# Two-layer masked attention on one core: layer 0's softmax sums counted once per half, layer 1's first accumulating DMA issued two steps later

## The chip, the cores and the metric

The kernel runs on one core of a Trainium2 chip. The metric is the device time of one execution in microseconds (us). The core has five engines with queues of their own, which work side by side and wait for one another through semaphores: TensorE (PE: matmuls; PEld is its weight load), VectorE (DVE), ScalarE (ACT), GpSimd (POOL) and SyncE (SP). In this kernel SP issues the plain DMAs, and GpSimd issues the loads of the adjacency matrix and the DMAs that add while they copy.

## What is computed

Sixteen graphs of 1024 nodes with 256 features go through two layers. Each layer normalizes its input, applies a ReLU, and adds masked attention to the input: 4 heads of 64 features in layer 0, 8 heads of 32 in layer 1. All is float32.

```python
# layer 0 (layer 1: 8 heads of 32, the same adjacency, with biases)
h = jnp.maximum(_layernorm(x, axis=-1), 0.0)
Q, K, V = ...                                   # per head
scores = jnp.einsum('bhne,bhme->bhnm', Q, K) * scale
scores = jnp.where(mask, scores, -jnp.inf)
attn = jax.nn.softmax(scores, axis=-1)
heads = jnp.einsum('bhnm,bhme->bhne', attn, V)
x = x + concat(heads) @ Wo.T + bo
```

## The kernel before

**Tiling.** For one graph and layer the 1024 queries fall into two halves of 512 (`qh`). The heads fall into two groups (`g`): a group holds 128 features, so two heads in layer 0 and four in layer 1. A group of a half is worked in steps, 4 in layer 0 and 8 in layer 1. A step computes four blocks of 128 keys x 512 queries: `scores` (TensorE, L447, into PSUM tiles `ps`), then `exponentials`: a mask operation on VectorE (L463) and an exponential on ScalarE (L469), giving the tile `p`; then, two steps later, `weigh` (TensorE, L481) multiplies `p` with the values into `po`. Layer 0 thus has 16 steps a graph and layer 1 has 32. The whole program is one list of 768 steps: layer 0 of graph b+1, then layer 1 of graph b, and so on. Below, *a* is the step at which layer 0 of a graph begins and *c* = a + 16 the one at which layer 1 of the graph before it begins.

**The sums of the softmax.** The exponentials are not divided by their sum at once. Tiles of a group are added up (layer 0: `add_tiles`, L490 to L496, on VectorE and GpSimd; layer 1: GpSimd, L582, for two tiles, and DMAs that add one pair into the other, `accumulate`, L568). Then `count` (L343) multiplies the result with ones on TensorE. This sums over the 128 partitions and leaves the sums of each head in `pz`, repeated over the head's rows. Layer 0 counts once a group, two matmuls of 64 columns; layer 1 counts a group in two counts, each four matmuls of 32 columns. After that come, by due times counted in steps from the end of the group:

- `spread`: ScalarE copies `pz` to `s`; small DMAs on SP deal a row of each head out over partitions (`sums`);
- `invert`: VectorE takes the reciprocal `vn` (L383), and a DMA puts it into DRAM (`vd`);
- `fetch`: DMAs on SP read it back, repeated over the rows of a head (`inv`);
- `normalize`: GpSimd multiplies the weighted values `cat` with `inv` (L399);
- `end_half`, after both groups: TensorE multiplies `cat` with the output weights (`py`, L429), and VectorE adds the rows (L434).

**What sets the order.** The order on each engine is written out by hand. `Stream.run` goes through the steps; in each it issues the scores of this step, the weighing of the step two earlier (put off by one step, where an even step has a large matmul block due), the counts due, the exponentials, the additions of layer 0, and then the other work due, in the order in which it was entered, with the large matmul blocks (`k`, `q`, `values`, `end_half`) last. `later(i, f)` enters work for step i. Every engine then runs its own queue in order. As GpSimd and SP wait only for what they need, they can be ahead of the step that TensorE is at, or behind.

For a layer 0 group that ends at step i, the count and the spread are due at i+4, then invert i+6, fetch i+7, normalize i+9, end_half i+11. The end is two steps after the last step's own number, so in a graph's layer 0 the counts fall at a+9, a+13, a+17 and a+21. In layer 1 the first accumulating DMA of a group is issued at the step of its fourth tile (`j == 3`), and the first count follows `waits[0]` steps later; in the first group that is the DMA at c+5 and the count at c+11.

**Buffers.** Three pairs of PSUM banks serve `ps`, `pq`, `pv` and `py` in turn, so that a new one waits for the reader of the one three back. Odd tiles `p` have two buffers and even ones seven: a mask operation of an odd step waits for the GpSimd addition (L582) that reads the tile two odd steps back. `pz` has one bank.

Of the kernel before, what the change touches and what calls it, by code (L numbers as in the profile page):

```python
# [10 lines left out]
F32 = mybir.dt.float32  # L11
# [7 lines left out]
P = 128  # L19
# [69 lines left out]
def fast_program(ctx, tc, a, w, loads, chk):  # L89
# [3 lines left out]
    nc = tc.nc  # L93
# [8 lines left out]
    work = ctx.enter_context(tc.tile_pool(name="work", bufs=2))  # L102
# [209 lines left out]
    class Group:  # L312


        def __init__(self, inp, mask, qh, g, half):
            self.inp, self.mask, self.qh, self.g, self.half = inp, mask, qh, g, half
            self.layer = inp.layer
            self.D = E // HEADS[self.layer]
            self.per = P // self.D
            self.scale = 1.0 / math.sqrt(self.D)  # L320
            self.n = f"{inp.n}_{qh}_{g}"
            self.n_f = self.per * 512 // P
            self.last = qh == QH - 1 and g == 1

            self.hurry = False

            self.waits = ((6, 6), (7, 7), (8, 6), None)[2 * qh + g]

            self.brief, self.pairs = self.last and inp.b == B - 2, False

# [7 lines left out]
        def count(self, p, start, stop):  # L338

            if start:  # L340
                self.s = ps_o.tile([P, 512], F32, tag="pz", name=f"pz_{self.n}")
            for r in range(self.per):
                nc.tensor.matmul(  # L343
                    self.s[r * self.D : (r + 1) * self.D, :], w.ones.to_broadcast([P, self.D]), p[:, r, :],
                    start=start, stop=stop,
                )

        def count_added(self):
            self.count(self.t, True, True)

        def copy_out(self):
            if self.g == 0:
# [5 lines left out]

        def spread(self):

            s = work.tile([P, 512], F32, tag="s", bufs=1, name=f"s_{self.n}")
            nc.scalar.copy(tiled(s), by_tile(self.s))  # L362
            inp, k = self.inp, 2 * self.qh + self.g
            if k == 0:

                pool, tag = small, f"sums{self.layer}"
                if self.layer and inp.b == B - 1:
                    pool, tag = adjp, "adj"
                inp.sums = pool.tile(
                    [P, 4 * self.n_f], F32, tag=tag, bufs=1, name=f"sums_{inp.n}"  # L370
                )
            self.sn = inp.sums[:, ts(k, self.n_f)]
            lanes = P // self.per
            for r in range(self.per):
                nc.sync.dma_start(
                    self.sn[r * lanes : (r + 1) * lanes, :],
                    s[r * self.D : r * self.D + 1, :].rearrange("r (c f) -> r c f", f=self.n_f),
                )

        def invert(self):  # L380

            vn = small.tile([P, self.n_f], F32, tag="vn", bufs=1, name=f"vn_{self.n}")
            nc.vector.reciprocal(vn, self.sn)  # L383
            vd = dram.tile([self.per, 512], F32, tag=f"vd{self.layer}", name=f"vd_{self.n}")
            nc.sync.dma_start(self.lanes(vd), vn)
            self.vd = vd

        def fetch(self):

            vd = self.vd  # L390
            self.inv = work.tile([P, 512], F32, tag="inv", bufs=1, name=f"inv_{self.n}")
            for r in range(self.per):
                nc.sync.dma_start(
                    self.inv[r * self.D : (r + 1) * self.D, :], vd[r].partition_broadcast(self.D)
                )

        def normalize(self):
            o = self.half.cat[:, self.g, :]
            nc.gpsimd.tensor_mul(o, o, self.inv)  # L399

        def finish(self):

            inp, qh = self.inp, self.qh
            inv = work.tile([P, 512], F32, tag="inv", bufs=1, name=f"inv_{self.n}")
            py = psum_pair(f"py_{self.n}").rearrange("p a (t e) -> p (a t) e", e=E)
            rows, cat = xs[inp.b, qh], self.half.cat
            dst = quarters(out, inp.b, qh)
            for h in range(2):
                q = ts(h, 256)
                nc.vector.reciprocal(tiled(inv)[:, ts(h, 2)], by_tile(self.s)[:, ts(h, 2)])  # L410
                nc.vector.tensor_mul(cat[:, self.g, q], cat[:, self.g, q], inv[:, q])
                for i in (2 * h, 2 * h + 1):
                    for c in range(2):
                        nc.tensor.matmul(
                            py[:, i, :], cat[:, c, ts(i, P)], w.o[self.layer][:, c, :],
                            start=(c == 0), stop=(c == 1),
                        )
            for h in range(2):
                t = ts(h, 2)
                nc.vector.tensor_add(rows[:, t, :], py[:, t, :], rows[:, t, :])  # L420
                for g in range(4):
                    nc.sync.dma_start(dst[g][:, t, :], rows[ts(g, 32), t, :])
# [84 lines left out]
    class Stream:  # L507
# [62 lines left out]
        def count_steps(self, i, st):  # L570


            gr, j = st.gr, st.j
            if gr.hurry and j >= NT - 2:
                if st.last:
                    self.counted(i, gr)
                gr.count(st.p, False, st.last)
            elif j % 2:
                one = self.steps[i - LEAD - 1].p
                if gr.last and not (gr.brief or gr.pairs) and j == 7:  # L580
                    self.accumulate(gr.two, gr.one)
                nc.gpsimd.tensor_add(one, one, st.p)  # L582
                if gr.pairs:
                    self.later(i + 2, gr.count, one, j == 1, st.last)
                elif j == 1:
                    gr.one = one
                elif j == 3:
                    self.accumulate(one, gr.one)
                    gr.one = one
                    if not gr.last:  # L590
                        self.later(i + gr.waits[0], gr.count, one, True, False)
                    if gr.brief:
                        self.later(i + 8, gr.count, one, True, False)
                elif gr.brief:
                    self.later(i + (6 if j == 5 else 4), gr.count, one, False, st.last)
                elif j == 5:
                    gr.two = one
                elif not gr.last:
                    self.accumulate(one, gr.two)
                    self.later(i + gr.waits[1], gr.count, one, False, True)  # L600
                else:
                    self.later(i + 1, self.accumulate, one, gr.two)
                    self.later(i + 4, gr.count, one, True, True)
# [7 lines left out]
        def end_group(self, i, gr):  # L611

            if gr.hurry:
                for f in (gr.spread, gr.finish, gr.inp.test):
                    self.later(i, f)
                return

            if gr.layer == 0:
                self.later(i + 4, gr.count_added)
                at = 4, 6, 7, 9, 11  # L620
            else:
                at = ((6, 12, 15, 19), (7, 12, 14, 17, 19), (6, 9, 11, 14), None)[2 * gr.qh + gr.g]
                if gr.pairs:
                    at = 2, 5, 6, 7, 9
                elif gr.last:
                    at = 4, 6, 7, 9, 11
            for k, f in zip(at, (gr.spread, gr.invert, gr.fetch, gr.normalize)):
                self.later(i + k, f)
            if gr.last:

                k = 7 if gr.layer or gr.inp.b == 0 else 37
                self.later(i + k if gr.inp.b + gr.layer < B - 1 else len(self.steps) + 2, gr.inp.test)
            if gr.g == 1:
                self.later(i + at[4], gr.end_half)
# [109 lines left out]
    for t in range(NT):  # L744
        i = 5 + 2 * t
# [8 lines left out]
    for b in range(B - 1):  # L754
# [14 lines left out]
        if b + 2 < B:  # L769
# [3 lines left out]
            if b == 0:  # L773
                norms(other, 0, a + 14, a + 15, c + 2, c + 3)
                block_inputs(other, 0, c + 4, c + 5, c + 6, c + 8, c + 16, c + 18)
                norms(other, 1, c + 3, c + 4, c + 6, c + 7)
                block_inputs(other, 1, c + 10, c + 12, c + 16, c + 22, c + 26, c + 30)
            else:
                norms(other, 0, a + 10, a + 12, a + 13, a + 15)
                block_inputs(other, 0, c, c + 1, c + 2, c + 8, c + 16, c + 18)  # L780
                norms(other, 1, c, c + 4, c + 5, c + 6, bias=c + 42)
                block_inputs(other, 1, c + 7, c + 8, c + 12, c + 22, c + 26, c + 30)
            for i, t in zip((9, 13, 17, 22, 33, 37, 41, 45), range(NT)):
                later(a + i - 5, mask.load, t)
# [260 lines left out]
```

## Time and profile before

| | |
|---|---|
| median of 3 runs | 3202.38 us (3201.98 to 3203.7) |
| profiled execution | 3201.31 us, of which the span of the core is 3199.5 us |
| granted TensorE clock | 0.997 of full speed |
| scores, L447 (PE) | 1134.1 us busy, 6144 matmul entries |
| weighing, L481 (PE) | 990.6 us busy, 6144 entries |
| counts, L343 (PE) | 196.1 us busy, 1248 entries |
| mask operation, L463 (DVE) | 1796.8 us busy, 1536 of 1212 ns |
| addition of two tiles, L582 (POOL) | 1171.3 us busy, 255 of 4596 ns |
| normalization, L399 (POOL) | 185.4 us busy, 127 of 1460 ns |
| issue of an accumulating DMA, L568 (POOL) | 133 of 882 ns (median) |

A row of the profile's groups reads: line, engine, operation, output<-input, shapes, count | busy us, mean ns of one | idle time of the engine just before, and what ended it. A row of a timeline reads: start in us, length, engine, line, operation, with the idle time before it and its releaser in square brackets. The times of matmuls overlap, since one begins before the last has drained, so what a block of them costs is read from the start of the next.

### The profile page before, as it was taken

The numbers are of one execution on the slowest core, as the hardware profiler recorded it, in microseconds if no ns is written. First come the engines' busy times: TensorE is split into PE (matmuls) and PEld (weight loads), VectorE is DVE, ScalarE is ACT, GpSimd is POOL, SyncE is SP. The second block draws the span as 40 slices with busy tenths as digits, with TensorE's granted clock in tenths as the row PEclk, the third lists the DMA queues.
The fourth block names the chain that finished last, engine by engine and source line by source line (L and its number), as shares of the span: only waits on it lengthen the run. The fifth ranks groups of instructions, "written<-read, shape, count | busy, mean of one in ns | idle before, by whom it ended". The sixth has DMA issues, their size and how long they took to land.

```text
span 3199.5 us, 44432 instructions
## 1 busy us (share of the span) xinstructions
PE 3153.7 (99%) x16662; PEld 1212.4 (38%) x16662; DVE 2532.5 (79%) x2786; ACT 2242.4 (70%) x2472; POOL 2352.4 (74%) x1103
## 2 busy tenths in 40 slices
PE   8999999999999999999999999999999999999998
PEld 3443433433334333333433334343343333333332
DVE  5677787887878888787887878878788887887776
ACT  5667677776767767677676776767777676775765
POOL 4567677786877868678686776877778687786776
PEclk9999999999999999999999999999999999999999
DMA  6326556364563645646465463655636456462321
GB/s 132 53 47 131 108 112 130 88 135 106 111 134 92 130 104 109 131 99 129 95 127 117 101 134 92 131 104 112 135 88 133 108 111 135 91 131 62 85 62 32
DMA packets 347792, 341.21 MB, mean 107 GB/s; under 512 B 196016, under 2 KB 290480, under 8 KB 330544
## 3 DMA queue, kind: packets, MB, share of 16 engines
q0 software_dynamic: 37584, 173.03, 29.2%
q1 hardware_dynamic: 309984, 165.26, 21.5%
q8 instruction: 133, 2.18, 0.3%
q14 instruction: 91, 0.75, 0.1%
HBM read 149.95 MB, written 47.96 MB: 62 GB/s over the span
## 4 chain that ended last, share of the span: by engine, by line
PE 89%; ACT 4%; DVE 3%; POOL 2%; issue 1%; DMA 1%; SPq 0%; DVEq 0%; POOLq 0%; ACTq 0%
PE ps L447 31%; PE po L481 27%; PE pq L266 13%; PE py L429 7%; PE pv L302 6%; PE pz L343 5%; DVE p L463 2%; ACT p L469 2%; ACT hn L210 1%; ACT mask L163 1%; POOL p L582 1%; POOL rstd L199 0%; ACT v L306 0%; DVE st L191 0%; DMA hT<-turned 0%
## 5 line engine op out<-in xcount | busy, mean ns | idle before, releaser
L463 DVE SCALAR_TENSOR_TENSOR p<-mask,ps 128x1024 f32<-128x1024 fp8e5 x1536 | 1796.8, 1212 | 461.3 <-PE ps L447 423.6
L469 ACT ACTIVATE p<-p 128x1024 f32<-128x1024 f32 x1536 | 1609.4, 1056 | 784.9 <-DVE p L463 745.4
L582 POOL TENSOR_TENSOR p<-p,p 128x2048 f32<-128x2048 f32 x255 | 1171.3, 4596 | 250.0 <-PE po L481 152.3
L447 PE MATMUL ps<-qT,kT 32*128 32x512 f32 (+1 forms) x6144 | 1134.1, 631 | 7.2 <-ACT v L306 4.4
L481 PE MATMUL po<-p,v 128*32 128x512 f32 (+1 forms) x6144 | 990.6, 601 | 2.1 <-ACT cat L354 1.8
L447 PEld LDWEIGHTS ps<-qT,kT 32*128 32x128 f32 (+1 forms) x6144 | 363.7, 184 | 706.2 <-issue 308.6
L494 POOL TENSOR_TENSOR p<-p 128x1024 f32<-128x1024 f32 x128 | 301.9, 2358 | 284.0 <-DVE p L493 275.3
L481 PEld LDWEIGHTS po<-p,v 128*32 128x32 f32 (+1 forms) x6144 | 229.2, 118 | 690.8 <-issue 500.3
L493 POOL TENSOR_TENSOR p<-p 128x1024 f32<-128x1024 f32 x64 | 150.8, 2357 | 173.3 <-DVE p L490 101.5
L266 PE MATMUL pq<-hT,wk 128*128 128x512 f32 x512 | 242.8, 618 | 8.9 <-DMA hT<-turned 6.3
L302 PE MATMUL pv<-wv,hT 128*128 128x256 f32 x1024 | 237.8, 385 | 0.0
L266 PE MATMUL pq<-hT,wq 128*128 128x512 f32 x512 | 236.6, 605 | 0.0
L429 PE MATMUL py<-wo,cat 128*128 128x256 f32 x1008 | 235.5, 386 | 0.5 <-POOL cat L399 0.2
L302 PEld LDWEIGHTS pv<-wv,hT 128*128 128x128 f32 x1024 | 189.4, 190 | 70.5 <-DVE p L463 30.4
L429 PEld LDWEIGHTS py<-wo,cat 128*128 128x128 f32 x1008 | 185.6, 190 | 72.5 <-issue 31.4
L343 PE MATMUL pz<-p,ones 128*32 128x512 f32 (+1 forms) x1248 | 196.1, 595 | 0.8 <-ACT s L362 0.8
L399 POOL TENSOR_TENSOR cat<-cat,inv 128x512 f32<-128x512 f32 x127 | 185.4, 1460 | 5.0 <-DMA inv<-vd 3.1
L219 POOL TENSOR_TENSOR x<-x,bo 128x1024 f32<-128x1024 f32 x64 | 152.1, 2376 | 15.8 <-DMA bo<-in_bo_dram 15.8
L490 DVE TENSOR_TENSOR p<-p 128x1024 f32<-128x1024 f32 x128 | 163.2, 1275 | 0.0
L210 ACT ACTIVATE hn<-x,shift,rstd 128x256 f32<-128x256 f32 x256 | 138.2, 588 | 24.9 <-DMA turned<-hn 17.7
L496 POOL TENSOR_TENSOR p<-p,p 128x1024 f32<-128x1024 f32 x64 | 151.5, 2367 | 5.0
L266 PEld LDWEIGHTS pq<-hT,wk 128*128 128x128 f32 x512 | 94.4, 194 | 153.3 <-issue 112.9
(51 smaller groups left out, 1665.4 us busy)
## 6 DMA issues: line engine op xcount, KB each, us to landing
p<-p POOLq DMA_DIRECT2D x133, 1024.0 KB, 7.7
adj<-in_adj_dram POOLq DMA_DIRECT2D x128, 256.0 KB, 4.2
turned<-hn SPq DMA_DIRECT2D x58, 512.0 KB, 2.9
hT<-turned SPq DMA_DIRECT2D x232, 128.0 KB, 3.1
x<-in_x_dram SPq DMA_DIRECT2D x128, 128.0 KB, 2.7
inv<-vd SPq DMA_DIRECT2D x128, 128.0 KB, 2.9
inv<-vd SPq DMA_DIRECT2D x252, 64.0 KB, 3.6
out_dram<-x SPq DMA_DIRECT2D x124, 128.0 KB, 2.4
```

The lines of the kernel that those rows point to most:

```text
L210: nc.scalar.activation(hn[:, ts(i, E)] if whole else self.blocks(half)[:, :, i, :], rows if whole else rows.rearrange("p (c q) -> p c q", ...
L266: nc.tensor.matmul(pq[:, m, :], wt[self.layer][:, c, ts(m, P)], self.hT[half][:, c, :], start=(c == 0), stop=(c == 1),)
L302: nc.tensor.matmul(pv[:, i, :], self.hT[half][:, c, ts(i, P)], w.v[self.layer][:, c, :], start=(c == 0), stop=(c == 1),)
L343: nc.tensor.matmul(self.s[r * self.D : (r + 1) * self.D, :], w.ones.to_broadcast([P, self.D]), p[:, r, :], start=start, stop=stop,)
L399: nc.gpsimd.tensor_mul(o, o, self.inv)
L429: nc.tensor.matmul(py[:, i, :], self.half.cat[:, c, ts(i, P)], w.o[self.layer][:, c, :], start=(c == 0), stop=(c == 1),)
L447: nc.tensor.matmul(st.ps[i // 2][:, i % 2, :], gr.inp.kT[r * D : (r + 1) * D, gr.g, ts(kt, P)], gr.inp.qT[gr.qh][r * D : (r + 1) * D, gr.g ...
L463: nc.vector.scalar_tensor_tensor(out=half, in0=gr.mask.m[gr.qh][:, kt, :].unsqueeze(1).to_broadcast([P, 2, 512]), scalar=-EDGE if gr.layer ...
L469: nc.scalar.activation(half, half, AF.Exp, scale=gr.scale)
L481: nc.tensor.matmul(gr.o[r * D : (r + 1) * D, :], gr.inp.v[:, kt, h * D : (h + 1) * D], st.p[:, i, :], start=(kt == 0), stop=(kt == NT - 1),)
L494: nc.gpsimd.tensor_add(a, a, b)
L582: nc.gpsimd.tensor_add(one, one, st.p)
```

## The change

Layer 0 now has one count for both groups of a half. The first group only leaves its added tile behind (`half.first`). When the second group ends, `count_added` multiplies the four head sums of the two tiles in one go: four matmuls of 32 columns, one for each head of the half. There is then one `spread`, one `invert` and one `fetch` for the half, the last with two `inv` tiles, and `normalize` does both groups one after the other. The due times become i+3 for count and spread, i+5 for invert, i+6 (first half) or i+5 (second half) for fetch, i+7 or i+6 for normalize, and end_half stays at i+11. So the counts fall at a+12 and a+20, and in the second half invert and fetch fall at c+6 and both normalizations at c+7.

In layer 1, for the first group of the first half, the first accumulating DMA is entered two steps later, at c+7, and so comes after both normalizations in GpSimd's queue. The count that reads it moves from c+11 to c+12. The copies `s` share the two buffers of `inv`, where each had one of its own. One addition of the bias rows to x (`add_bias`, L219) is due at c+36, not c+42.

```diff
@@ -319,12 +319,12 @@
             self.per = P // self.D
             self.scale = 1.0 / math.sqrt(self.D)
             self.n = f"{inp.n}_{qh}_{g}"
-            self.n_f = self.per * 512 // P
+            self.n_f = 16
             self.last = qh == QH - 1 and g == 1
 
             self.hurry = False
 
-            self.waits = ((6, 6), (7, 7), (8, 6), None)[2 * qh + g]
+            self.waits = ((7, 6), (7, 7), (8, 6), None)[2 * qh + g]
 
             self.brief, self.pairs = self.last and inp.b == B - 2, False
 
@@ -339,14 +339,14 @@
 
             if start:
                 self.s = ps_o.tile([P, 512], F32, tag="pz", name=f"pz_{self.n}")
-            for r in range(self.per):
+            for r, of in enumerate(p if type(p) is list else [p[:, r, :] for r in range(4)]):
                 nc.tensor.matmul(
-                    self.s[r * self.D : (r + 1) * self.D, :], w.ones.to_broadcast([P, self.D]), p[:, r, :],
-                    start=start, stop=stop,
+                    self.s[ts(r, 32), :], w.ones.to_broadcast([P, 32]), of, start=start, stop=stop
                 )
 
         def count_added(self):
-            self.count(self.t, True, True)
+            both = self.half.first.t, self.t
+            self.count([t[:, r, :] for t in both for r in range(2)], True, True)
 
         def copy_out(self):
             if self.g == 0:
@@ -358,50 +358,53 @@
 
         def spread(self):
 
-            s = work.tile([P, 512], F32, tag="s", bufs=1, name=f"s_{self.n}")
+            s = work.tile([P, 512], F32, tag="inv", name=f"s_{self.n}")
             nc.scalar.copy(tiled(s), by_tile(self.s))
-            inp, k = self.inp, 2 * self.qh + self.g
+            inp, k = self.inp, 2 * self.qh + self.g if self.layer else self.qh
             if k == 0:
 
                 pool, tag = small, f"sums{self.layer}"
                 if self.layer and inp.b == B - 1:
                     pool, tag = adjp, "adj"
                 inp.sums = pool.tile(
-                    [P, 4 * self.n_f], F32, tag=tag, bufs=1, name=f"sums_{inp.n}"
+                    [P, (4 if self.layer else 2) * self.n_f], F32, tag=tag, bufs=1,
+                    name=f"sums_{inp.n}",
                 )
             self.sn = inp.sums[:, ts(k, self.n_f)]
-            lanes = P // self.per
-            for r in range(self.per):
+            for r in range(4):
                 nc.sync.dma_start(
-                    self.sn[r * lanes : (r + 1) * lanes, :],
-                    s[r * self.D : r * self.D + 1, :].rearrange("r (c f) -> r c f", f=self.n_f),
+                    self.sn[ts(r, 32), :],
+                    s[32 * r : 32 * r + 1, :].rearrange("r (c f) -> r c f", f=self.n_f),
                 )
 
         def invert(self):
 
             vn = small.tile([P, self.n_f], F32, tag="vn", bufs=1, name=f"vn_{self.n}")
             nc.vector.reciprocal(vn, self.sn)
-            vd = dram.tile([self.per, 512], F32, tag=f"vd{self.layer}", name=f"vd_{self.n}")
+            vd = dram.tile([4, 512], F32, tag="vd", name=f"vd_{self.n}")
             nc.sync.dma_start(self.lanes(vd), vn)
             self.vd = vd
 
         def fetch(self):
 
-            vd = self.vd
-            self.inv = work.tile([P, 512], F32, tag="inv", bufs=1, name=f"inv_{self.n}")
-            for r in range(self.per):
-                nc.sync.dma_start(
-                    self.inv[r * self.D : (r + 1) * self.D, :], vd[r].partition_broadcast(self.D)
-                )
+            self.inv = {}
+            for g in (self.g,) if self.layer else range(2):
+                inv = self.inv[g] = work.tile([P, 512], F32, tag="inv", name=f"inv_{self.n}_{g}")
+                for r in range(self.per):
+                    nc.sync.dma_start(
+                        inv[ts(r, self.D), :],
+                        self.vd[r if self.layer else 2 * g + r].partition_broadcast(self.D),
+                    )
 
         def normalize(self):
-            o = self.half.cat[:, self.g, :]
-            nc.gpsimd.tensor_mul(o, o, self.inv)
+            for g, inv in self.inv.items():
+                o = self.half.cat[:, g, :]
+                nc.gpsimd.tensor_mul(o, o, inv)
 
         def finish(self):
 
             inp, qh = self.inp, self.qh
-            inv = work.tile([P, 512], F32, tag="inv", bufs=1, name=f"inv_{self.n}")
+            inv = work.tile([P, 512], F32, tag="inv", name=f"inv_{self.n}")
             py = psum_pair(f"py_{self.n}").rearrange("p a (t e) -> p (a t) e", e=E)
             rows, cat = xs[inp.b, qh], self.half.cat
             dst = quarters(out, inp.b, qh)
@@ -585,7 +588,10 @@
                 elif j == 1:
                     gr.one = one
                 elif j == 3:
-                    self.accumulate(one, gr.one)
+                    if gr.qh or gr.g:
+                        self.accumulate(one, gr.one)
+                    else:
+                        self.later(i + 2, self.accumulate, one, gr.one)
                     gr.one = one
                     if not gr.last:
                         self.later(i + gr.waits[0], gr.count, one, True, False)
@@ -616,8 +622,11 @@
                 return
 
             if gr.layer == 0:
-                self.later(i + 4, gr.count_added)
-                at = 4, 6, 7, 9, 11
+                if gr.g == 0:
+                    gr.half.first = gr
+                    return
+                self.later(i + 3, gr.count_added)
+                at = (3, 5, 5, 6, 11) if gr.qh else (3, 5, 6, 7, 11)
             else:
                 at = ((6, 12, 15, 19), (7, 12, 14, 17, 19), (6, 9, 11, 14), None)[2 * gr.qh + gr.g]
                 if gr.pairs:
@@ -778,7 +787,7 @@
             else:
                 norms(other, 0, a + 10, a + 12, a + 13, a + 15)
                 block_inputs(other, 0, c, c + 1, c + 2, c + 8, c + 16, c + 18)
-                norms(other, 1, c, c + 4, c + 5, c + 6, bias=c + 42)
+                norms(other, 1, c, c + 4, c + 5, c + 6, bias=c + 36)
                 block_inputs(other, 1, c + 7, c + 8, c + 12, c + 22, c + 26, c + 30)
             for i, t in zip((9, 13, 17, 22, 33, 37, 41, 45), range(NT)):
                 later(a + i - 5, mask.load, t)
```

## What I expect, written before the changed kernel ran

> **What bounds the kernel now.** I read the page first: the engine totals, then the chain that ended last.
>
> ```profile
> PE 3153.7 (99%) x16662; PEld 1212.4 (38%) x16662; DVE 2532.5 (79%) x2786; ACT 2242.4 (70%) x2472; POOL 2352.4 (74%) x1103
> ...
> PE 89%; ACT 4%; DVE 3%; POOL 2%; issue 1%; DMA 1%; SPq 0%; DVEq 0%; POOLq 0%; ACTq 0%
> ```
>
> TensorE works 99% of the span and carries 89% of the last chain; no other engine is above 79%. So a TensorE microsecond taken out is gained, and a wait put into TensorE's queue is lost, wherever no second limit stands close behind. Next the groups of instructions on TensorE with shapes kept apart:
>
> ```profile
> L481 PE MATMUL po<-p,v 128*64 128x512 f32 x2048 | 478.7, 601 | 0.0
> ...
> L343 PE MATMUL pz<-p,ones 128*32 128x512 f32 x992 | 129.5, 594 | 0.8 <-ACT s L362 0.8
> L343 PE MATMUL pz<-p,ones 128*64 128x512 f32 x256 | 66.5, 598 | 0.0
> ```
>
> The trace records two entries for one float32 matmul. The 256 entries 64 columns wide are layer 0's counting: 64 groups, two matmuls each, 66.5/64 = 1.04 us a group. The 992 entries 32 columns wide are layer 1's: 124 counts of four matmuls, 129.5/124 = 1.04 us. Four 32-wide matmuls cost what two 64-wide ones cost. What a count really takes is the distance to the next start, as the timeline of one batch shows (start, us, engine, line):
>
> ```profile
> 1003.31 3.65 PE L481 MATMUL po<-p,v 128*64 128x512 f32 x16
> 1006.79 1.03 PE L343 MATMUL pz<-p,ones 128*64 128x512 f32 x4
> 1007.75 1.14 PE L447 MATMUL ps<-qT,kT 32*128 32x512 f32 x8
> ```
>
> That is 1007.75 - 1006.79 = 0.96 us. Over all 64 the mean of this distance is 0.97 us, for layer 1's counts of four 0.98.
>
> Last I read the stretch that the second part of the change touches, steps c+11 and c+12 (c is the step at which layer 1 of a batch begins): TensorE, then GpSimd, then one line of VectorE.
>
> ```profile
> 1041.46 1.42 PE L447 MATMUL ps<-qT,kT 32*128 32x512 f32 x8
> 1042.81 1.06 PE L481 MATMUL po<-p,v 128*32 128x512 f32 x8
> 1043.69 1.04 PE L343 MATMUL pz<-p,ones 128*32 128x512 f32 x8
> 1044.67 1.14 PE L447 MATMUL ps<-qT,kT 32*128 32x512 f32 x8
> 1045.79 3.69 PE L429 MATMUL py<-wo,cat 128*128 128x256 f32 x16
> ```
>
> ```profile
> 1027.29 0.94 POOL L568 DMA_DIRECT2D p<-p  x1 [0.31 <-POOL p L582]
> 1027.96 1.58 POOL L399 TENSOR_TENSOR cat<-cat,inv 128x512 f32<-128x512 f32 x1
> 1031.07 4.55 POOL L582 TENSOR_TENSOR p<-p,p 128x2048 f32<-128x2048 f32 x1 [1.53 <-PE po L481]
> 1038.69 4.57 POOL L582 TENSOR_TENSOR p<-p,p 128x2048 f32<-128x2048 f32 x1 [3.08 <-PE po L481]
> ```
>
> ```profile
> 1043.29 2.35 DVE L463 SCALAR_TENSOR_TENSOR p<-mask,ps 128x1024 f32<-128x1024 fp8e5 x2 [0.46 <-POOL p L582]
> ```
>
> The first accumulating DMA is issued at 1027.29, and the count that needs it runs at 1043.69: some 9 us of cover after a landing in 7.0 us. VectorE at step c+11 waited for the GpSimd addition that ended at 1043.26. The page's row for this DMA:
>
> ```profile
> p<-p POOLq DMA_DIRECT2D x133, 1024.0 KB, 7.7
> ```
>
> **What the Trainium skill says.** "TensorEngine Tiling (Array Packing)", Tiling Modes: with 128 rows the array splits into two tiles of 64 columns or four of 32, which run in parallel. The trace agrees (0.97 against 0.98 us a count). "TensorE: Matmul & The Clock Gate", Part 3, The mechanism: matmuls start and end strictly in program order, so a count that waits holds everything behind it. "DMA: Bandwidth & Descriptors", SWDGE vs HWDGE vs iDMA: a DMA that accumulates can only be issued by GpSimd; here each takes 0.88 us of GpSimd's queue, and it stands in that queue behind whatever is put ahead.
>
> **The change part by part**
>
> *Counts of layer 0.* Before, a half has two counts (each two matmuls of 64 columns), after it one (two heads from each group, four of 32). 16 batches x 2 halves = 32 counts go: 32 x 0.97 = 31.0 us. The 32 that stay cost 0.01 more each, 0.2 us. The removed ones stood at a+9 and a+17 (a is where layer 0 starts). TensorE must not run into another limit there: the smallest distances between VectorE's release of a PSUM buffer and its next use in the steps after them are 2.2 us (a+10 to a+13) and 1.7 us (a+18, a+19); one of 0.47 us, for the py at a+20, is widened by the count put ahead of it. So the 31 us are real at these places.
>
> *One step sooner.* The remaining counts go from a+13 to a+12 and from a+21 to a+20, there ahead of py. Their tiles must be added by then: GpSimd ends that addition (L496) at 975.8 and 1013.2 in the batch shown, and TensorE reaches the counts at about 978.9 and 1015.5 (979.82 and 1016.47 less the 0.97 gained). Covers of 3.1 and 2.3 us; cost nothing. If they went, each microsecond late would cost 16 to a side.
>
> *Copies, reciprocals, DMAs.* 32 ScalarE copies and 32 VectorE reciprocals go, which neither bounds. On SP a half has four spreading DMAs as before, one vd instead of two, four inv as before, now in one burst of about 0.55 us of queue each. With invert at c+6 I put vd on SP at 1027.8, landing 1.5 to 2.4 us later, and the last inv issue near 1031.6; 2.9 us of flight give 1034.5 for the last, the first pair 1033. GpSimd asks at 1035.6. For the first half invert follows x loads and a mask flip on SP, and its inv should land by 1003 where GpSimd asks at 1005.7. Both normalizations (1.25 us each between starts) fit in GpSimd's idle 2.69 us before 1008.41. Cost nothing, with 2 us of cover. The shared "inv" pair of buffers adds a wait of a copy for normalizations four or more steps old: nothing. The bias addition of 2.4 us moves into GpSimd idle time: nothing.
>
> *The accumulating DMA.* This is where something is lost. All clock times here are on the scale of the old trace; the 0.97 gained before shifts everything alike. At c+7 GpSimd runs the third L582, which TensorE releases, until 1035.62, then two normalizations (2 x 1.25, to 1038.1), and only then issues the DMA. So it leaves at 1038.05 instead of 1027.29. It takes 7.0 us when alone (this place in most batches), 7.5 to 8.2 where other traffic runs beside it; here the last part of the hT<-turned blocks runs beside it (SP issues until 1039.9). I take 7.7: it lands at 1045.75, 0.2 to the wait, 1045.95.
>
> The count moves from c+11 to c+12, between ps and py. With it gone from c+11, the next ps could start at 1043.69, and its count at 1044.76. Two things are late. First, the second half of that ps needs the PSUM buffer of VectorE's first operation at c+11. That waits for the fourth L582, which now starts behind the DMA issue (1038.05 + 0.88 = 1038.9 to 1039.0, not 1038.69): VectorE is done at 1044.8, ps at 1045.4, 0.65 us late. Second, the DMA, 1045.95. The later one decides: the count starts 1.2 us late, and py behind it. The addition of py on VectorE waits for py and the next exponentials for it, so nothing catches up. Bounds: 0.65 us if the DMA takes 7.0; 3.0 us at the 9.5 us that rare transfers show.
>
> In 13 like batches (1 to 13) this costs 13 x 1.25 = 16.2 us. Batch 0 has 4.8 us of slack on the DMA and pays only the buffer, 0.4. In batch 14 GpSimd is busy back to back and py already waited on VectorE: about 0.8. Batch 15 counts by pairs and has no such DMA.
>
> *Sum.* -31.0 + 0.2 + 16.2 + 0.4 + 0.8 = -13.4 us. The profiled execution took 3201.31 us (span 3199.5), so 3188; the median of the runs shown is 1.1 above it, so 3189.
>
> **The rivals**
>
> *The DMA is hidden.* It lands in 7.0 us, or the ring of buffers is less tight than I think, and the count waits 0 to 0.7 us. For it: the isolated transfers. Against it: 0.65 us already follow from the L582. Then 3202.4 - 30.8 + 13 x 0.35 + 1 = 3177 (3171.6 with no loss at all).
>
> *Gain and loss cancel.* The DMA needs 8.4 us: the wait is 1.9 us, 13 x 1.9 = 24.7, so 3197 to 3198. For it: 8.1 to 8.5 us in single batches of the trace. Against it: those lie beside loads of adj, absent here.
>
> *Slower.* The inv burst lands after 1035.6, or the accumulation meets the hT blocks in full, so that it lands 9.4 us after the 1038.05 I assume: the count is 2.9 us late, 13 x 2.9 + 1.2 = 38.9, against 30.8: 3210.5. It turns slower than before when the count is over 2.3 us late, that is a landing past 1046.85. For it: SP's queue is in order, and a flip waits up to 14.9 us there for its adj. Against: that flip (c+2) ends at 1018.9, before the spread needs the queue.
>
> *Not what it says.* If four 32-wide matmuls on two different tiles did not run side by side, the gain would be gone: 3217. Layer 1's form is the same; I give it almost nothing.
>
> **How the numbers follow.** The forecast (count 0.9 to 1.7 us late, 3184 to 3195): 0.50. Hidden: 0.21. Cancelled, 3196 to 3208: 0.18. Slower: 0.11. Range 3174 to 3204, leaving out half of the slower case and the lower end of the hidden one. No change is within 0.2%, 6.4 us, about what a measurement of this kernel can tell; so faster means below 3196: 0.50 + 0.21 less the forecast's upper edge, 0.70. Same 0.19, slower 0.11.
>
> **What would show it.** pz 64 wide gone, pz 32 wide at 992 + 256 = 1248 entries, some 163 us. No wait at the counts of a+12 and a+20. Between ps and pz at c+12 a gap of about half a microsecond, released by the DMA p<-p, and the L568 after two L399. If that gap is nil, the hidden case holds; if L399 there waits for inv, the slower one. I am wrong if TensorE idles after the removed counts, or if GpSimd's additions reach a+20 late.

## The result, and the profile after

The changed kernel takes 3210.14 us (median of 12 runs, 3206.65 to 3213.53) against 3202.49 us (median of 12, 3200.94 to 3205.46): a ratio of 1.0025, with a 95% interval of 1.0017 to 1.0033. It is slower, and the forecast of 3189 us lies on the wrong side. The profiled execution took 3207.03 us, its span is 3205.3, which is 5.8 more than before. It is the second fastest of the 12, so what follows accounts for these 5.8 us and not for the 3 us by which the median lies above it.

The engine totals, the chain that ended last and the counts' group of the changed kernel, from its page:

```profile
PE 3156.0 (98%) x16662; PEld 1208.3 (38%) x16662; DVE 2543.8 (79%) x2754; ACT 2216.2 (69%) x2440; POOL 2353.4 (73%) x1103
...
PE 83%; ACT 4%; DMA 4%; DVE 4%; POOL 2%; issue 2%; SPq 1%; DVEq 0%; POOLq 0%; ACTq 0%
...
L343 PE MATMUL pz<-p,ones 128*32 128x512 f32 x1248 | 164.0, 598 | 4.3 <-DMA p<-p 3.0 <-ACT s L362 0.8 <-POOL p L585 0.4
```

The counts did what was said: no 64-wide ones are left, and 1248 entries take 164.0 us where all the counts took 196.1. Yet TensorE is busy 2.3 us longer. So some 34 us of "busy" time went in elsewhere, most of it into the scores, which take 1162.4 us (1134.1 before). A wait between two matmuls of one block hides there: the end of a matmul in the trace is modelled, and the next start is late only by fractions of a us, which the trace does not show as idle time. I therefore laid the start times of the scores of all 768 steps side by side. A batch here is the layer 0 of one graph and the layer 1 of the graph before it, 48 steps; batches 1 to 13 are alike. In these the kernels differ only in the following stretches (median over the 13, in us, worked out from the starts of the score matmuls):

| steps | before | changed | difference |
|---|---|---|---|
| a+9 (count removed) | 6.36 | 5.50 | -0.86 |
| a+12 and a+13 (count moved) | 12.05 | 12.07 | +0.01 |
| a+17 (count removed) | 5.51 | 4.66 | -0.86 |
| a+18 and a+19 | 7.65 | 8.59 | +0.94 |
| a+20 and a+21 (count moved) | 8.65 | 8.64 | -0.01 |
| c+11 and c+12 (count moved, DMA later) | 7.95 | 9.26 (mean 9.54) | +1.31 (mean +1.58) |

Two places gain 1.72 us a batch and two others lose 2.26, or 2.53 on the mean. Here is the first loss in the timeline of the changed kernel, the same batch as in the prediction: VectorE, then GpSimd, then TensorE.

```profile
1000.61 2.29 DVE L493 TENSOR_TENSOR p<-p 128x1024 f32<-128x1024 f32 x1
1003.00 2.11 DVE L496 TENSOR_TENSOR p<-p 128x1024 f32<-128x1024 f32 x1
1005.04 2.34 DVE L466 SCALAR_TENSOR_TENSOR p<-mask,ps 128x1024 f32<-128x1024 fp8e5 x2
```

```profile
1000.55 3.48 POOL L402 TENSOR_TENSOR cat<-cat,inv 128x512 f32<-128x512 f32 x2
1005.19 2.35 POOL L497 TENSOR_TENSOR p<-p 128x1024 f32<-128x1024 f32 x1 [1.16 <-DVE p L496]
```

```profile
1006.47 2.09 PE L450 MATMUL ps<-qT,kT 32*128 32x512 f32 x8
1008.49 1.92 PE L484 MATMUL po<-p,v 128*32 128x512 f32 x16
```

The additions of layer 0 on VectorE, whose median in this kernel is 1.22 us, take 2.29 and 2.11 us here: they run exactly beside the two normalizations (L402), which take 3.48 us together instead of 2.5. The same place in the kernel before, VectorE and then GpSimd:

```profile
1005.78 1.22 DVE L490 TENSOR_TENSOR p<-p 128x1024 f32<-128x1024 f32 x1
1007.11 1.23 DVE L493 TENSOR_TENSOR p<-p 128x1024 f32<-128x1024 f32 x1
```

```profile
1008.41 2.36 POOL L494 TENSOR_TENSOR p<-p 128x1024 f32<-128x1024 f32 x1 [2.69 <-DVE p L493]
```

There GpSimd was idle during most of the two additions, waiting for them. In the changed kernel, VectorE reaches the mask operation (L466) late, frees the PSUM buffer late, and the scores at a+19 take 2.09 us instead of 1.14. No idle time is shown on TensorE. One sees it in the length of the block alone.

The second loss, at c+11 and c+12: TensorE, then GpSimd, then VectorE.

```profile
1036.39 1.43 PE L450 MATMUL ps<-qT,kT 32*128 32x512 f32 x8
1037.75 1.06 PE L484 MATMUL po<-p,v 128*32 128x512 f32 x8
1038.74 2.19 PE L450 MATMUL ps<-qT,kT 32*128 32x512 f32 x8
1040.97 1.06 PE L343 MATMUL pz<-p,ones 128*32 128x512 f32 x8
```

```profile
1030.52 2.49 POOL L402 TENSOR_TENSOR cat<-cat,inv 128x512 f32<-128x512 f32 x2
1032.96 0.94 POOL L571 DMA_DIRECT2D p<-p  x1
1033.64 4.86 POOL L585 TENSOR_TENSOR p<-p,p 128x2048 f32<-128x2048 f32 x1
```

```profile
1038.53 3.48 DVE L466 SCALAR_TENSOR_TENSOR p<-mask,ps 128x1024 f32<-128x1024 fp8e5 x3 [0.76 <-POOL p L585]
```

The order on GpSimd is as forecast: two normalizations, then the DMA, then the fourth addition, which ends 0.3 us later than in the old pattern (2.1 us, not 1.8, after the start of step c+11) and holds VectorE. But most of the lost time is inside the block of scores (2.19 us instead of 1.14), not between scores and count. The count does wait for the DMA, though not for long. The view of this DMA, issued at 1032.96 (two of its lines):

```profile
  PEld pz L343: 0.9, 1
...
DMA to landing us min/median/max: 8.0/8.0/8.0
```

It lands at 1040.9, and the count starts right behind it, at 1040.97. From the start of the last score matmul to that of the count it is 0.52 to 0.93 us in 12 of the 13 batches, where 0.52 is no wait, and 2.28 us in one (batch 8), where the DMA takes 9.6 us. Behind that count, batch 8 also has 3.4 us in which TensorE was granted half its clock.

### The profile page after: what moved, and what is told of

It reads as the page before. It is cut to its first block, busy times and chain, and to the rows that moved or that the text cites. A ratio compares the mean times of both kernels' runs of the same rounds, so it can differ in the third digit from the quotient of the medians.

```text
span 3205.3 us, 44270 instructions
## 1 busy us (share of the span) xinstructions
PE 3156.0 (98%) x16662; PEld 1208.3 (38%) x16662; DVE 2543.8 (79%) x2754; ACT 2216.2 (69%) x2440; POOL 2353.4 (73%) x1103
## 4 chain that ended last, share of the span: by engine, by line
PE 83%; ACT 4%; DMA 4%; DVE 4%; POOL 2%; issue 2%; SPq 1%; DVEq 0%; POOLq 0%; ACTq 0%
PE ps L450 29%; PE po L484 25%; PE pq L266 11%; PE py L432 7%; PE pv L302 6%; PE pz L343 4%; DVE p L466 3%; DMA p<-p 2%; ACT p L472 2%; POOL p L585 1%; ACT hn L210 1%; DMA inv<-vd 1%; POOL cat L402 1%; ACT mask L163 1%; DMA vd<-vn 0%
## 5 line engine op out<-in xcount | busy, mean ns | idle before, releaser
L466 DVE SCALAR_TENSOR_TENSOR p<-mask,ps 128x1024 f32<-128x1024 fp8e5 x1536 | 1797.4, 1214 | 419.5 <-PE ps L450 371.8
L450 PE MATMUL ps<-qT,kT 32*128 32x512 f32 (+1 forms) x6144 | 1162.4, 632 | 10.1 <-ACT v L306 4.4
L450 PEld LDWEIGHTS ps<-qT,kT 32*128 32x128 f32 (+1 forms) x6144 | 371.7, 184 | 729.8 <-issue 331.7
L497 POOL TENSOR_TENSOR p<-p 128x1024 f32<-128x1024 f32 x128 | 302.1, 2360 | 230.5 <-DVE p L496 225.5
L402 POOL TENSOR_TENSOR cat<-cat,inv 128x512 f32<-128x512 f32 x127 | 176.0, 1396 | 8.2 <-DMA inv<-vd 6.5
L493 DVE TENSOR_TENSOR p<-p 128x1024 f32<-128x1024 f32 x128 | 173.8, 1358 | 0.0
L343 PE MATMUL pz<-p,ones 128*32 128x512 f32 x1248 | 164.0, 598 | 4.3 <-DMA p<-p 3.0
L219 POOL TENSOR_TENSOR x<-x,bo 128x1024 f32<-128x1024 f32 x64 | 153.1, 2393 | 16.5 <-DMA bo<-in_bo_dram 16.5
L437 DVE TENSOR_TENSOR x<-py,x 128x1024 f32<-128x1024 f32 x63 | 77.1, 1224 | 96.8 <-PE py L432 96.8
## 6 DMA issues: line engine op xcount, KB each, us to landing
adj<-in_adj_dram POOLq DMA_DIRECT2D x128, 256.0 KB, 4.2
```

Source lines behind the costliest of these rows:

```text
L343: nc.tensor.matmul(self.s[ts(r, 32), :], w.ones.to_broadcast([P, 32]), of, start=start, stop=stop)
L402: nc.gpsimd.tensor_mul(o, o, inv)
L450: nc.tensor.matmul(st.ps[i // 2][:, i % 2, :], gr.inp.kT[r * D : (r + 1) * D, gr.g, ts(kt, P)], gr.inp.qT[gr.qh][r * D : (r + 1) * D, gr.g ...
L466: nc.vector.scalar_tensor_tensor(out=half, in0=gr.mask.m[gr.qh][:, kt, :].unsqueeze(1).to_broadcast([P, 2, 512]), scalar=-EDGE if gr.layer ...
L493: nc.vector.tensor_add(a, a, b)
L497: nc.gpsimd.tensor_add(a, a, b)
```

## The experiments

My theory after seeing this: (1) the normalizations beside VectorE's additions cost the 0.94 us at a+19; (2) at c+12 the count waits for the late DMA; (3) a removed count is worth 0.86 us. The rivals are with each run.

**1. Undo the DMA part.**

```diff
-            self.waits = ((7, 6), (7, 7), (8, 6), None)[2 * qh + g]
+            self.waits = ((6, 6), (7, 7), (8, 6), None)[2 * qh + g]
...
-                    if gr.qh or gr.g:
-                        self.accumulate(one, gr.one)
-                    else:
-                        self.later(i + 2, self.accumulate, one, gr.one)
+                    self.accumulate(one, gr.one)
```

> The changed kernel with the DMA part undone: the first accumulating DMA again at c+5, ahead of the normalizations, and its count again at c+11. Theory (the count at c+12 waits for the late DMA, 1.2 to 1.6 us a batch, more in batches 0 and 8): steps c+11 and c+12 together take 7.0 to 7.3 us more of nothing, that is 7.95 us as before the change instead of 9.2, and the time falls by about 22 us to 3188 (14 x 1.35 and some 3 us more). Rival (the normalizations at c+7 and the buffer ring hold TensorE there, not the DMA): the two steps stay near 9.2 us and the time near 3210. In both, steps a+18 and a+19 stay at 8.6 us.

Measured: 3214.24 us, ratio 1.0038 (1.0024 to 1.0052). The two steps take 9.63 us, mean 10.10. The theory missed: with the DMA back at c+5 the kernel is no faster. Run 3 shows why. Steps a+18 and a+19 stayed at 8.59.

**2. The first half's normalizations one step later.**

```diff
-                at = (3, 5, 5, 6, 11) if gr.qh else (3, 5, 6, 7, 11)
+                at = (3, 5, 5, 6, 11) if gr.qh else (3, 5, 6, 8, 11)
```

> The changed kernel with the first half's two normalizations at a+17 (behind the last addition of layer 0 in GpSimd's queue) instead of a+16. Theory (the two normalizations run at the same time as VectorE's additions L493 and L496 and slow them from 1.22 to 2.1 to 2.3 us, so that TensorE waits at a+19): the additions take 1.22 us again, steps a+18 and a+19 fall from 8.6 to about 7.65 us, 14 x 0.95 = 13 us, 3197. Rival (VectorE is late there because the count came a step sooner or was removed at a+17, so the order on TensorE is the cause): the additions may shorten but the two steps stay at 8.6 and the time at 3210. Steps c+11 and c+12 stay near 9.2 us in both.

Measured: 3194.75 us, ratio 0.9975 (0.9965 to 0.9985). The timeline of VectorE in the same batch:

```profile
1001.40 1.22 DVE L493 TENSOR_TENSOR p<-p 128x1024 f32<-128x1024 f32 x1
1002.73 1.23 DVE L496 TENSOR_TENSOR p<-p 128x1024 f32<-128x1024 f32 x1
```

The additions are back at 1.22 us and the two steps at 7.65. This one number in the due times is worth 15 us at the median (13 us at these two steps in the traces), and the loss at a+19 is explained: counts and their order on TensorE were not touched.

**3. Both edits.**

> Both of these edits: the counts of layer 0 merged, the DMA at c+5, the first half's normalizations at a+17. Theory: the losses at a+19 and at c+12 are separate and add, so what is left is the gain of the removed counts, 0.80 and 0.83 us a batch: 32 x 0.81 = 26, 3202.5 - 26 = 3176 to 3180. Rival (the two losses cover one another, time freed at one place is waited away at the other): not below 3186.

Measured: 3199.22 us, ratio 0.9991 (0.9984 to 0.9997); a+18 and a+19 take 7.65, c+11 and c+12 9.35 (mean 10.01). Slower than run 2, so in the merged kernel the DMA at c+5 does harm. The timeline of GpSimd and the row of the four inv transfers of this batch, first of this run, then of the changed kernel, show how:

```profile
1026.45 0.94 POOL L571 DMA_DIRECT2D p<-p  x1 [0.31 <-POOL p L585]
1029.26 4.55 POOL L585 TENSOR_TENSOR p<-p,p 128x2048 f32<-128x2048 f32 x1 [1.88 <-ACT mask L163]
1035.72 2.52 POOL L402 TENSOR_TENSOR cat<-cat,inv 128x512 f32<-128x512 f32 x2 [1.91 <-DMA inv<-vd]
1038.20 4.56 POOL L585 TENSOR_TENSOR p<-p,p 128x2048 f32<-128x2048 f32 x1
...
DMA to landing us min/median/max: 5.9/7.2/7.8
```

```profile
DMA to landing us min/median/max: 3.0/3.0/3.1
```

The 1 MB DMA and the four inv transfers now fall together. The transfers land 7.2 us after their issue (3.0 in the changed kernel), and each takes 1.25 us of SP to issue (median, 0.54 before). GpSimd waits for them, its fourth addition is late, VectorE waits for that, and TensorE for VectorE. The theory missed here too, at 3199 where it had 3176 to 3180. So the later DMA of the change does answer a real need that the merged fetch at c+6 creates.

**4. The DMA part alone, in the kernel before.** The same lines as in run 1, the other way round.

> The kernel before with the DMA part alone: the first accumulating DMA at c+7 and its count at c+12. Here the normalizations are at c+6 and c+10, so only one is ahead of the DMA and it falls into idle time: the DMA leaves right behind the third L582 and lands about 1 us ahead of the count. Theory (the wait comes from the DMA behind both normalizations): steps c+11 and c+12 grow by the buffer ring alone, 0.3 to 0.4 us from 7.95, and the time by about 5 us to 3207. Rival (any delay of this DMA by two steps makes the count wait): 9 us and over for the two steps, 3220. Second rival (the place of the count costs nothing): 7.95 us, 3202.

Measured: 3207.84 us, ratio 1.0020 (1.0012 to 1.0027); the two steps take 8.82 us. The timeline of TensorE:

```profile
1037.90 1.43 PE L447 MATMUL ps<-qT,kT 32*128 32x512 f32 x8
1039.26 1.06 PE L481 MATMUL po<-p,v 128*32 128x512 f32 x8
1040.25 1.90 PE L447 MATMUL ps<-qT,kT 32*128 32x512 f32 x8
1042.08 1.06 PE L343 MATMUL pz<-p,ones 128*32 128x512 f32 x8
```

The direction is as the theory said, but the step is over twice its size: +0.87 us, not 0.3 to 0.4. That the time came out near its 3207 was luck. In the trace the two steps lose 13.5 us over the 15 batches; the span grows by only 6.4, since batch 0 gains 6.5 us elsewhere, at step c+8 (see *Sum* in the next section). The DMA is issued at 1032.00 here and lands 8.8 us later, 1.3 us ahead of the count (in batches 8 and 9 it is late and the count waits). The 0.87 is the block of scores at c+12, 1.90 instead of 1.14. In the list of single matmuls its first pair starts at 1040.25 and the second only at 1041.03, when VectorE has released its buffer (one of the three pairs of PSUM banks that go round, the ring of buffers). The second pair then runs by itself for 1.05 us. The four score matmuls of a step lie in different rows of the array and run side by side in 1.07 us; as two pairs apart they take almost twice that.

**5 and 6. The DMA ahead of the normalizations at c+7, with the count at c+11 or c+12.** Both contain the edit of run 2, and run 5 also the edit of `waits` of run 1. The issue moves into the step of the third addition, behind it and ahead of everything due:

```diff
-                        self.later(i + 2, self.accumulate, one, gr.one)
+                        gr.first = one, gr.one
...
                 elif j == 5:
                     gr.two = one
+                    if not (gr.qh or gr.g):
+                        self.accumulate(*gr.first)
```

> The counts of layer 0 merged, the first half's normalizations at a+17, and the first accumulating DMA at c+7 ahead of both normalizations (right behind the third addition L585), its count at c+11. The inv tiles have then landed before the DMA begins. Theory: DMA issue about 5.8 us before step c+11 begins, landing 7.0 to 7.8 us after it, 0.2 to 1 us ahead of the count; normalizations wait for nothing; steps c+11 and c+12 take 7.95 us as before the change. What is left is the gain, 0.85 us for each removed count: 32 x 0.85 = 27, 3175 to 3178. Rival (the inv fetch and the DMA disturb each other in any order): GpSimd waits for inv or the count for the DMA, the two steps over 9 us, time over 3190.

> The same with the count at c+12. Here the DMA lands about 2 us ahead of its count, so any time lost at c+12 is not the DMA's. Theory (the count taken from c+11 lets TensorE reach the scores of c+12 before VectorE has freed their buffer; the two pairs of score matmuls then run one after the other, 1.05 us each, not side by side): steps c+11 and c+12 take 8.8 us as in the run with the DMA part alone, 14 x 0.87 = 12 us more than the count at c+11, 3187 to 3190. Rival (the loss at c+12 is the wait for the DMA): 7.95 us and the same time as with the count at c+11.

Measured: count at c+11: 3178.13 us, ratio 0.9925 (0.9909 to 0.9942), the two steps 8.29 us. Count at c+12: 3189.98 us, ratio 0.9965 (0.9951 to 0.9979), the two steps 9.11 us. Both runs have the same DMA at the same place; the count one step later costs 12 us, though its tile has landed 1.1 to 2.1 us before in the 13 like batches. (These batches account for 8.5 us of the 12 in the traces, and batch 0 for 4.0, with a stretch at half clock in it, so the forecast of 12 was met in part by luck.) So the place of the count, not the wait for the DMA, makes most of the loss at c+12. The 0.34 us over 7.95 with the count at c+11 (0.51 on the mean) is a wait for the DMA: it takes 8.4 us at the median, not the 7.0 to 7.8 of the theory, and in each of the 13 batches the count starts 0.04 us behind its landing. This version beats both kernels.

**7. One normalization beside one addition, in the kernel before.**

```diff
-                at = 4, 6, 7, 9, 11
+                at = 4, 6, 7, 9 if gr.qh or gr.g else 11, 11
```

> The kernel before, with one normalization alone (first half, first group) moved from a+14 to a+16, into the idle time of GpSimd before the addition L494 of step a+17. Theory (a GpSimd multiply and a VectorE addition of float32 in SBUF at the same time slow one another): VectorE's L490 at a+17 takes about 2.3 us instead of 1.22, the next addition L493 stays near 1.3, VectorE is about 1 us later and TensorE has 1.7 us of room at a+19, so the time stays at 3202. Rival (what slowed the additions was something else in the merged kernel): 1.22 us both.

Measured: 3201.52 us, ratio 1.0001 (0.9991 to 1.0010). VectorE, then GpSimd:

```profile
1005.26 1.94 DVE L490 TENSOR_TENSOR p<-p 128x1024 f32<-128x1024 f32 x1
1007.30 1.23 DVE L493 TENSOR_TENSOR p<-p 128x1024 f32<-128x1024 f32 x1
```

```profile
1004.83 1.28 POOL L399 TENSOR_TENSOR cat<-cat,inv 128x512 f32<-128x512 f32 x1
```

The normalization began first and kept its 1.28 us, to 1006.11. The addition ended at 1007.20, which is 1.09 us after that: it hardly advanced while GpSimd worked. In nine other batches, where the two overlap longer, the addition takes 2.13 to 2.32 us, as the theory said. The trace of the kernel before says the same: 15 of its 192 additions of layer 0 on VectorE take over 1.3 us, up to 2.60, and exactly these overlap an operation of GpSimd. One such collision is covered by the room at a+19 in the kernel before. The changed kernel has two, and less room, as the count at a+17 is gone.

**8. The count at c+13, in the changed kernel.** `(7, 6)` in `waits` becomes `(8, 6)`.

> The changed kernel with the first count of layer 1's first group at c+13, one step later still. The DMA has then landed 3 us or more ahead of it. Theory (ring of buffers at c+12, with the DMA the smaller part): steps c+11 to c+13 together, 12.2 us in the changed kernel against 10.9 before the change, stay at 11.8 to 12.2. Rival (the wait for the DMA is the loss): they fall to 10.9 to 11.2, and the time by 15 us to 3195.

Measured: 3204.41 us, ratio 1.0005 (0.9998 to 1.0012). Steps c+11 to c+13 take 12.02 us; in the changed kernel 12.19 (mean 12.46), before it 10.88. With the DMA out of the question 1.14 of the 1.31 us are still there. The rest of the mean is 0.43 us: 0.3 is what the count waits for the DMA, unevenly over batches, and 0.1 the stretch at half clock in batch 8.

**9 and 10. What a count is worth.** In `count_added` of the kernel before, the count is called twice; in run 10 as one accumulation, `(True, False)` then `(False, True)`.

> The kernel before with each of layer 0's 64 counts run twice in a row (the second overwrites the first with the same sums). Theory (a count taken out or put in beside matmuls of the same tiling is worth 0.86 us; the other 0.1 us of the 0.97 to the next start is the change of tiling, which stays): steps a+9, a+13, a+17 and a+21 each grow by 0.86 us, 64 x 0.86 = 55, 3257. Rival (a count is worth its whole 0.97 us): 62, 3264.

> The kernel before with each of layer 0's 64 counts run twice, the second time added to the first in the same accumulation, so that nothing waits for the first to drain (layer 0's sums come out doubled, its attention halved; the work is otherwise the same). Theory (a count put in or taken out beside matmuls of the same tiling is worth 0.86 us, and the other 0.1 us of the 0.97 to the next start is the change of tiling): steps a+9, a+13, a+17 and a+21 each grow by 0.86 us, 64 x 0.86 = 55, 3257. Rival (a count is worth its whole 0.97 us): 62, 3264.

Run 9 gave 3271.98 us, ratio 1.0218 (1.0188 to 1.0248): each of the four steps grew by 1.15 us, which neither theory has. The second count started 0.66 us behind the last pair of the first, where accumulating pairs follow at 0.43; it overwrites the same PSUM bank, and I take it that it had to wait until the first had left it. So this run says nothing on the question. Run 10 has no such restart: 3252.55 us, ratio 1.0156 (1.0127 to 1.0186), and each of the four steps grew by 0.86 us. The total of 50 us is below 55 since other steps got a little shorter, among them 0.11 to 0.14 us in most of the a+12. So a count is worth 0.86 us, the same as was measured where it was taken out.

## Why the prediction failed, by its own steps

*Counts of layer 0*: the mechanism was right, the term mis-sized. I took 0.97 us to the next start for the worth of a count. It is 0.86, and the other 0.1 is the change of the array's tiling, which stays when the count goes. The trace of before shows it: 16 entries of weighing, 64 columns wide, take 3.48 us to the next start where a count 64 wide follows, and 3.58 where scores or a count 32 wide follow. 32 counts are 27.5 us, not 31.0.

*One step sooner*: right. The sums of a+12 with a+13 and of a+20 with a+21 did not move by more than 0.02 us, and no count waited for GpSimd's additions.

*Copies, reciprocals, DMAs*: here is the sentence that failed, "Both normalizations (1.25 us each between starts) fit in GpSimd's idle 2.69 us before 1008.41. Cost nothing". GpSimd was idle there because it waited for VectorE's additions, which fill this very gap (1005.78 and 1007.11 above), and an addition with two inputs in SBUF hardly advances beside a GpSimd operation on SBUF (run 7). The Trainium skill has this: "SBUF — State Buffer", section SBUF: two separate sides, says that VectorE and GpSimd share a pair of SBUF ports under an exclusive lock, held for the whole instruction, when VectorE's operation has two inputs in SBUF and GpSimd's reads SBUF. Run 7 agrees with it: in 0.85 us of overlap the addition advanced by about 0.13. The forecast put this term at nothing; it cost 0.94 us in 13 batches and 1.1 in batch 0, 13.4 us, and run 2 gets nearly all of it back (13.0 in the trace). The estimates for SP and the inv burst held: landing in 3.0 us, no wait of GpSimd for it in this batch (6.5 us in four places of the whole span).

*The accumulating DMA*: the mechanism held, and the sum came near, 1.25 us forecast and 1.31 found at the median; but one of its two terms was mis-sized. The DMA left 3.4 us before the start of step c+11, as forecast, and landed after 8.0 us at the median (7.7 forecast). "The later one decides", with the DMA as the later, held in 11 of the 13 batches: there the count starts 0.04 us behind the landing. But the other term, the ring of buffers, is nearly as late by itself, 1.16 us (run 6) where I had 0.65. So taking the DMA out of the way gives back only 0.15 us at the median (the changed kernel less run 6). The 1.16 is 0.87 when the count leaves c+11 (run 4) and 0.29 more when the fourth addition stands behind the normalizations (run 6 less run 4; it ends 0.3 us later in run 6). I had let a late pair of score matmuls take the 0.53 us that it takes beside the other pair; alone it takes 1.05.

The mean of 1.58 over 13 batches makes 20.6 us where I had 16.2. Batch 0 lost 2.8 us, not 0.4: there a bias addition of 2.6 us stands behind the DMA in GpSimd's queue, so that the fourth addition ends at 256.0 and VectorE's mask operation waits for it. Batch 14 lost 1.2, not 0.8.

*Sum*: by parts it is -27.5 + 13.4 + 20.6 + 2.8 + 1.2 = +10.5 us, where the forecast had -13.4. Of these 24 us, 13.4 are the normalizations, 7.2 the DMA part and 3.3 the counts. The profile shows +5.8, as the forecast also missed a gain, 6.5 us at step c+8 of batch 0. TensorE there, before and changed:

```profile
249.33 5.95 PE L266 MATMUL pq<-hT,wk 128*128 128x512 f32 x8 [4.13 <-DMA hT<-turned]
```

```profile
242.92 3.70 PE L266 MATMUL pq<-hT,wk 128*128 128x512 f32 x8
```

The old trace waits for the hT<-turned transfer and then has a stretch at half clock; this step takes 11.15 us before and 4.70 in the changed kernel. It takes 4.70 in runs 1 to 6 and 8 as well, so either part of the change removes the wait, and 10.6 to 11.6 in runs 7, 9 and 10, which have neither. Why was not tested. Another 2.2 us less in batch 14, and 3.9 more in the last graph's layer 1 and at the two ends of the program, where short stretches at half clock fall differently in the two traces, close the sum.

The slower rival ended near the measured time (3210.5), but by luck: its mechanism, a DMA landing 9.4 us after its issue, was not what happened, as this DMA took 8.0 us at the median and over 9 in one batch of the 13. The figure of the last rival, 3217, comes to 3220 if batches 0 and 14 are put in as in the forecast.

What stays open: why the DMA takes 7.1 us at c+5 and 8.0 to 8.8 at the later places, why the wait in batch 0 goes, and whether the DMA could be placed so that the last 0.34 us of run 5 goes too.

## What to carry to other kernels

Idle time of an engine is free room only if you know what it waits for: when it waits for a neighbour that shares its memory ports, work put there delays the very thing it waits for. Price a removed block by the change in distance between the blocks around it, not by its distance to the next start, and price a late matmul of a side-by-side group at its length alone. Where a transfer is moved out of the way of others, look for a place between them before paying with the order of the engine that needs it: ahead of the normalizations and behind the fetch, the same DMA let its count stay at c+11, and the two steps lost 0.34 us a batch instead of 1.31. And when a run lands on its forecast, add up its steps all the same: run 4 did so because a loss of 13.5 us met a gain of 6.5 that nobody had foreseen.

## What the runs showed that I had not expected

- A float32 addition on VectorE (1.22 us alone) takes up to 2.3 us beside a GpSimd multiply (1.94 in the batch shown); the mask operation, with one input in PSUM, kept its 1.21 us beside GpSimd's L497.
- Two pairs of score matmuls in different rows of the array: 1.07 us side by side, 1.05 us each when the second pair must wait for its buffer.
- Four transfers of 128 KB land in 3.0 us with no accumulating DMA in flight, and in 7.2 us in the batch shown when one of 1 MB was issued ahead of them, and SP's issue of each grows from 0.54 to 1.25 us.
- Starting a new sum in a PSUM bank right behind the last one costs 0.29 us more than going on with it (1.15 against 0.86 us a count).
